# The values products moved up behind the scores in thirteen rows of a cross-attention and FFN kernel

## The chip, the cores and the metric

The kernel runs on one NeuronCore of a Trainium2 chip. The metric is the device time of one launch in microseconds (us), the median over the runs shown. TensorE (PE) multiplies, VectorE (DVE), ScalarE (ACT) and GpSimd (POOL) do the rest of the arithmetic, and transfers are issued from SyncE's queue (SP). Each engine works through its own list of instructions in order; semaphores tie the lists together.

## The reference

One decoder layer over 16 sequences of 64 tokens, 1024 tokens of width 512: cross-attention with 32 heads of 128, then a dense layer with a routed low-rank addition. Cut to what matters:

```python
q = (layernorm(x) @ Wq).reshape(b, 64, 32, 128)
k = (ctx @ Wk).reshape(b, 64, 32, 128)
v = (ctx @ Wv).reshape(b, 64, 32, 128)
score = einsum('bqhd,bkhd->bhqk', q, k) / sqrt(128) + position_bias
score = where(mask, score, -inf)
probs = where(mask, softmax(score), 0)
x = x + einsum('bhqk,bkhd->bqhd', probs, v).reshape(b, 64, 4096) @ Wo
h = layernorm(x)
x = x + h @ base_W.T + base_b + lora(h, top-k softmax of h @ router_W.T)
```

[...]

## The kernel before

**Precision and blocks.** A float32 operand is split into a high part (ACT casts it, L70) and a low part (DVE subtracts, L71), and each product is three matmuls: high by high, high by low, low by high. The three projections use Strassen-Winograd sums: seven products of halves in place of eight, in the order of `ORDER` = 1, 2, 6, 5, 7, 4, 3 (L37).

**Stages.** First the keys and values of all heads are computed and written to DRAM (up to about 320 us of the span). Then comes the attention loop over the 16 head pairs (`for p in range(NP)`, L607), here called rows: row p with p = 0 is the first. Last comes the dense layer (from L680).

**A row.** The program of a row is a string of letters, `steps` (L608), read from left to right:

- `S` (L617): the scores of the row's pair. For each of the two heads 16 matmuls of 128x64 tiles into a bank of their own pool (L470; the profile counts two records for each), then DVE adds the bias (L473) and takes the maxima (L475). In rows 1 to 14 that pair is p. The first head's exponentials, eight activations of 64 columns on ACT (L481), follow at once; the second head's are recorded at the fifth `Q`.
- `Q` (L625): one of the seven Winograd products of the next pair's queries, six matmuls of 512 columns (L259). Products 1, 6, 7 and 4 add up in one PSUM bank, called x; product 2 fills bank z, products 5 and 3 fill bank y. After products 1, 6 and 7 ACT copies bank x to SBUF (`u`, L554) before the next product is added onto it; after product 4 it copies the result out (L561). DVE forms the other three results (L565).
- `P` (L612): the values products of the pair before (`pv_mm`, L510): 64 matmuls of 64x64 tiles (128 records, L517) into four banks, from `pt`, the turned probabilities, and `v`. Each bank is split by ACT (cast to `oh`, L70) and DVE (`ol`, L71). The next four `v` tiles are loaded into the same buffers behind it.
- `O` (L671): one eighth of the output projection of that pair (`proj_o`, L527): six matmuls of 512 columns, then DVE adds the bank to `acc` (L534).
- `h` (L661): the second head's softmax is finished behind the last `O`: normed on DVE (L487 to L489), transposed on DVE (L498), copied by ACT to `pt` (L500), and four transfers put the off-diagonal quarters in place (L505). The first head's is finished at the fifth `Q`.

The fifth `Q` also loads the output weights for the next row (`load_o`, L448: `so` by DMA, split into `wh` on ACT and `wl` on DVE), and the seventh loads and splits the query weights for the pair after next (`gh`, `gl`).

**Order.** PE's list is the order of recording. The lists of ACT, DVE, POOL and SP are put together by a scheduler from the recording, its own estimates, `issue_after` (not ahead of a named instruction) and `high_priority(offset=SOON)`, which holds for the splits of the values banks, the copies of Winograd banks and the additions to `acc`. The general PSUM pool has six banks (L61), the pool of the scores two.

## Time and profile before

| | |
|---|---|
| median of 3 runs | 763.34 us (763.02 to 763.68) |
| profiled execution: span from the first to the last instruction | 761.7 us |
| between the span and the median | 1.6 us |
| PE, DVE, ACT, POOL busy | 752.5, 565.8, 412.0, 194.8 us |
| granted TensorE clock over the span | 0.999 |
| one row of the loop (537.93 to 562.83) | 24.90 us |

The profiled execution is known by its span alone; what lies around the span is taken as the 1.6 us by which the median exceeds it. A timeline line reads: start, duration, engine, source line, operation, output and inputs with their shapes, the count of merged instructions, and in brackets the idle time before it with what ended it. The duration of a matmul includes its way through the array, so that starts, not ends, show the rate: in a run of 512-column matmuls one starts every 0.227 us. The same holds on ACT and DVE, where the next instruction starts some 0.1 us before the former one's recorded end.

### The profile page before, as it was taken

The page shows a single profiled execution, that of the slowest core. Times are in us where ns is not written, and L with a number is a line of the kernel's source. Part 1 is how long each engine was busy: PE and PEld are TensorE (multiplying, and loading weights), DVE is VectorE, ACT ScalarE, POOL GpSimd, SP SyncE. Part 2 cuts the span into 40 slices and gives each one's busy share as a digit, 9 for nine tenths or more (in the row PEclk, how much of TensorE's full clock was granted, in tenths as well). Part 3 has the DMA queues.
Part 4 walks back from the last instruction along what each step waited for, and adds up shares of the span by engine and source line. Part 5 has one row for each costly group of instructions (what it writes and reads, how often), then busy time and mean ns, then how long its engine had stood idle before and what let it go on. Part 6 is the DMA issues. An engine that isn't in the chain of part 4 may idle for free.

```text
span 761.7 us, 16780 instructions
## 1 busy us (share of the span) xinstructions
PE 752.5 (99%) x6154; PEld 624.9 (82%) x6154; DVE 565.8 (74%) x1076; ACT 412.0 (54%) x1157; POOL 194.8 (26%) x271
## 2 busy tenths in 40 slices
PE   8999999999999999999999999999999999999998
PEld 6888888888788888877888888888888888888898
DVE  7986567666655776869778777787778777878975
ACT  5654444444444445667645565456645765474361
POOL 0000008108820693223220222022211232010330
PEclk9999999999999999999999999999999999999999
DMA  6685647465735446466554465436544564462011
GB/s 255 229 285 186 205 157 229 147 218 179 224 130 187 156 126 225 142 222 217 189 158 149 138 199 167 142 120 201 174 141 134 180 185 140 125 199 84 1 57 56
DMA packets 84946, 126.79 MB, mean 166 GB/s; under 512 B 11776, under 2 KB 35072, under 8 KB 84864
## 3 DMA queue, kind: packets, MB, share of 16 engines
q1 hardware_dynamic: 80624, 123.56, 49.9%
q0 software_dynamic: 4096, 2.11, 1.2%
q8 instruction: 48, 0.79, 0.5%
q14 instruction: 34, 0.28, 0.1%
q10 hardware_dynamic: 144, 0.06, 0.0%
HBM read 83.74 MB, written 35.65 MB: 157 GB/s over the span
## 4 chain that ended last, share of the span: by engine, by line
PE 91%; DVE 3%; POOL 2%; DMA 2%; issue 1%; ACT 0%; SPq 0%; DVEq 0%; ACTq 0%; POOLq 0%
PE ps L259 73%; PE yz L259 5%; PE ps L742 5%; PE ps L517 4%; PE pss L470 4%; POOL xT L333 1%; DMA cT<-in_ctxT 1%; DMA so<-in_wo 0%; DMA xT<-xb 0%; DVE bs L708 0%; DVE gl L71 0%; PE pt L104 0%; DVE s L161 0%; DVE ol L71 0%; POOL st L711 0%
## 5 line engine op out<-in xcount | busy, mean ns | idle before, releaser
L481 ACT ACTIVATE p<-p,nm 128x64 f32<-128x64 f32 x256 | 85.9, 339 | 33.3 <-DVE nm L475 31.0
L534 DVE TENSOR_TENSOR acc<-acc,ps 128x512 f32<-128x512 f32 x128 | 86.8, 681 | 21.2 <-PE ps L259 20.4
L259 PE MATMUL ps<-wh,ol 128*128 128x512 f32 x256 | 99.9, 390 | 0.8 <-DVE ol L71 0.8
L259 PE MATMUL ps<-wh,oh 128*128 128x512 f32 x256 | 100.1, 391 | 0.0
L259 PE MATMUL ps<-wl,oh 128*128 128x512 f32 x256 | 99.7, 389 | 0.0
L70 ACT CAST gh<-s 128x512 fp32r<-128x512 f32 (+1 forms) x128 | 64.4, 514 | 56.0 <-PE ps L259 45.7
L333 POOL DMA_DIRECT2D xT<-xb x128 | 69.7, 552 | 84.9 <-DVE xb L330 80.7
L71 DVE TENSOR_TENSOR gl<-s,gh 128x512 fp32r<-128x512 f32 (+1 forms) x128 | 72.0, 566 | 23.2 <-ACT gh L70 23.1
L161 POOL TENSOR_TENSOR s<-rq 128x256 f32<-128x256 f32 x32 | 25.3, 790 | 238.9 <-DMA rq<-in_wq 190.1
L71 DVE TENSOR_TENSOR ol<-ps,oh 128x512 fp32r<-128x512 f32 x64 | 39.9, 683 | 31.5 <-ACT oh L70 31.3
L70 ACT CAST gh<-raw 128x512 fp32r<-128x512 f32 x48 | 29.8, 623 | 52.8 <-PE yz L259 36.1
L259 PEld LDWEIGHTS ps<-wh,ol 128*128 128x128 f32 x256 | 48.1, 188 | 11.4 <-DVE ol L71 1.6
L259 PEld LDWEIGHTS ps<-wl,oh 128*128 128x128 f32 x256 | 48.1, 188 | 10.0
L259 PEld LDWEIGHTS ps<-wh,oh 128*128 128x128 f32 x256 | 48.0, 188 | 10.0
L71 DVE TENSOR_TENSOR gl<-raw,gh 128x512 fp32r<-128x512 f32 x48 | 35.1, 731 | 27.9 <-ACT gh L70 20.7
L461 POOL TENSOR_TENSOR bm<-bm,maskb 128x512 f32<-128x512 f32 x32 | 42.4, 1348 | 36.6 <-DMA bm<-in_fside 36.6
L481 ACT ACTIVATION_READ_ACCUMULATOR p<-p,nm 128x1 f32 x256 | 48.6, 190 | 0.0
L565 DVE TENSOR_TENSOR q<-u,ps 128x512 f32<-128x512 f32 x48 | 32.8, 683 | 20.4 <-PE ps L259 16.0
L70 ACT CAST oh<-ps 128x512 fp32r<-128x512 f32 x64 | 33.2, 590 | 11.0 <-PE ps L517 11.0
L70 ACT CAST gh<-rq 128x256 fp32r<-128x256 f32 x48 | 19.5, 406 | 36.0 <-PE ps L259 32.1
L517 PEld LDWEIGHTS ps<-pt,v 64*64 64x64 f32 x2048 | 31.9, 135 | 5.7 <-issue 5.6
L554 ACT COPY u<-ps 128x512 f32<-128x512 f32 x48 | 27.9, 581 | 15.9 <-PE ps L259 8.8
(258 smaller groups left out, 1986.2 us busy)
## 6 DMA issues: line engine op xcount, KB each, us to landing
kd<-c SPq DMA_DIRECT2D x64, 256.0 KB, 2.6
vd<-c SPq DMA_DIRECT2D x64, 256.0 KB, 2.8
kT<-kd SPq DMA_DIRECT2D x64, 256.0 KB, 3.9
v<-vd SPq DMA_DIRECT2D x64, 256.0 KB, 3.7
raw<-in_wk SPq DMA_DIRECT2D x32, 256.0 KB, 4.0
raw<-in_wv SPq DMA_DIRECT2D x32, 256.0 KB, 4.3
rq<-in_wq SPq DMA_DIRECT2D x32, 256.0 KB, 4.1
bm<-in_fside SPq DMA_DIRECT2D x32, 256.0 KB, 4.5
```

Of the source, the lines that this page charges most:

```text
L70: first = nc.scalar.copy(hi, src)
L71: return first, (lo_eng or nc.vector).tensor_tensor(lo, src, hi.bitcast(F32), ALU.subtract)
L259: nc.tensor.matmul(o, lhsT=a, rhs=b, start=first and n == 0, stop=last and n == 2, skip_group_check=True)
L333: nc.gpsimd.dma_start(out=dst[32 * j:32 * j + 32, :, 32 * i:32 * i + 32], in_=xb[32 * i:32 * i + 32, j])
L461: nc.gpsimd.tensor_tensor(bm, bm, maskb, ALU.add)
L470: nc.tensor.matmul(ps[a * S:(a + 1) * S, t, :], lhsT=qT[n // 8][:, cq], rhs=kT[m // 8][:, ck], start=True, stop=True)
L481: nc.scalar.activation(p[:, t, :], p[:, t, :], AF.Exp, bias=nm[:, t:t + 1], accum_out=sme[:, t:t + 1])
L517: nc.tensor.matmul(ps[a][d:d + S, t * S:(t + 1) * S], lhsT=v[t // 2][r, t % 2, c], rhs=pt[r, :, t, :], start=True, stop=True)
L534: return nc.vector.tensor_tensor(acc[:, t, :], acc[:, t, :], ps, ALU.add)
L554: copy = nc.scalar.copy(s[i], b["x"])
L565: add = nc.vector.tensor_tensor(self.blocks[key], s[u], b[bk], ALU.add)
L742: nc.tensor.matmul(o, lhsT=a, rhs=b, start=start, stop=stop, skip_group_check=True)
```

## The change

The strings of rows 2 to 14 (the third to the fifteenth) are new. Row 1 keeps the old string, rows 0 and 15 are not touched.

```diff
-                steps = ("QSQQQQQQt" if p == 0 else "SQQQPQQOOQOhOQOOOO" if p + 2 < NP else
-                         "SQQQPQQOQQfSeeOOOOOhh" if p + 1 < NP else "PooOOOOOOO")
+                steps = ("QSQQQQQQt" if p == 0 else "SQQQPQQOOQOhOQOOOO" if p == 1 else
+                         "SPQQQQOOQOhQOQOOOO" if p + 2 < NP else
+                         "SPQQQQQOQQfSeeOOOOOhh" if p + 1 < NP else "PooOOOOOOO")
```

`P` moves from behind the third `Q` to a place directly behind `S`. In rows 2 to 13 the fifth `Q` (product 7) moves behind two `O`, so that what hangs on it (the second head's exponentials, the first head's softmax, the output weights) is recorded later by two `O`. `h` still stands behind the third `O`, now with one `Q` fewer ahead of it, and the sixth and seventh `Q` stand behind it, each with an `O` after. In row 14 only `P` moves. The count of every letter in a row is unchanged.

On ACT the scheduler's order changes with it. Before, a row runs: four exponentials of the first head, the copy of product 1, four exponentials, the copy of product 6, four casts of the values banks, two of the output weights. After: six exponentials, a cast, an exponential, a cast, an exponential, two casts of the values banks, one cast of the output weights, and then the copy of product 1; the other cast of the output weights and the copy of product 6 follow. On SP the first transfer of output weights moves from ahead of the eight `pt` transfers to between the two groups of four.

## Prediction

> **What bounds the kernel now.** I read the page's busy shares first, then the chain of work that ended last in order of time, then the timelines of PE and ACT over one row, and last the one place where PE waited for a copy out of an accumulating bank.

> ```profile
> PE 752.5 (99%) x6154; PEld 624.9 (82%) x6154; DVE 565.8 (74%) x1076; ACT 412.0 (54%) x1157; POOL 194.8 (26%) x271
> ```
> ```profile
> 538.00 2.02 PE pss L470 x64
> 540.02 4.32 PE ps L259 x18
> 544.34 2.04 PE ps L517 x128
> 546.38 16.52 PE ps L259 x72
> ```

> PE is busy for 99% of the span, and the chain of a row holds PE work only: 24.90 us = 2.02 (`S`) + 4.32 (three `Q`) + 2.04 (`P`) + 16.52 (four `Q`, eight `O`). No other engine is on the path, so a row gets shorter only where PE itself loses time, and any PE wait lengthens it in full. Where PE loses time is seen in its timeline:

> ```profile
> 537.61 0.39 PE L259 MATMUL ps<-wl,oh 128*128 128x512 f32 x1
> 537.93 2.09 PE L470 MATMUL pss<-kT,q 128*64 128x64 f32 x64
> 539.95 0.50 PE L259 MATMUL ps<-t1h,gh 128*128 128x512 f32 x1
> 540.28 0.39 PE L259 MATMUL ps<-t1h,gl 128*128 128x512 f32 x1
> ...
> 543.95 0.39 PE L259 MATMUL ps<-t6l,gh 128*128 128x512 f32 x1
> 544.27 2.11 PE L517 MATMUL ps<-pt,v 64*64 64x64 f32 x128
> 546.31 0.50 PE L259 MATMUL ps<-t5h,gh 128*128 128x512 f32 x1
> 546.65 0.39 PE L259 MATMUL ps<-t5h,gl 128*128 128x512 f32 x1
> ```

> The usual step between starts is 0.227 us. Going into small tiles it is 0.32 (537.61 to 537.93, 543.95 to 544.27), so 0.09 is lost; coming out it is 0.33 or 0.34, so about 0.10 is lost. A row pays four such changes. Of ACT's list in the same row:

> ```profile
> 540.69 0.35 ACT L481 ACTIVATE p<-p,nm 128x64 f32<-128x64 f32 x1 [2.42 <-DVE nm L475]
> ...
> 542.04 0.56 ACT L554 COPY u<-ps 128x512 f32<-128x512 f32 x1
> ...
> 545.47 2.06 ACT L70 CAST oh<-ps 128x512 fp32r<-128x512 f32 x4 [0.45 <-PE ps L517]
> 547.41 1.15 ACT L70 CAST wh<-so 128x512 fp32r<-128x512 f32 x2
> ```

> The exponentials start 2.76 us after the row's first score (540.69 less 537.93) and wait only for the maxima. The copy of product 1 comes after four of them, at 542.04, and ends at 542.60, just ahead of product 6 at 542.80, which is added onto the same bank and may not start before. That edge of 0.20 us is the point of the whole change.

> ```profile
> 193.37 0.58 ACT L230 COPY u<-ps 128x512 f32<-128x512 f32 x1
> 193.99 0.50 PE L259 MATMUL ps<-t4h,gh 128*128 128x512 f32 x1 [1.34 <-ACT u L230]
> ```

> Here, in the keys' stage, PE did wait for such a copy. It started 0.04 us after the copy's end, and its second matmul came at 194.33, 0.34 later: a restart costs 0.11.

> **The change, part by part.** Times are from the row's first score.

> *`P` behind `S`, on PE.* One way out of small tiles (0.10) and one way in (0.09) go; the step from 128x64 to 64x64 tiles comes. The trace does not show that step. It lies between 0 (the steps inside each section lose nothing) and 0.20 (both edges); nearest is a way in, 0.09, which I take. `P` starts at 2.02 + 0.09 = 2.11, product 1 at 4.15 (2.04 later), and lasts 0.34 + 5 x 0.227 = 1.47; product 2 lasts 1.36. Product 6 is then due at 6.98.

> *The copy of product 1, on ACT.* Its bank is full at about 5.9, but in the new order six exponentials, four casts of values banks, two exponentials and one cast of output weights stand ahead of it. From the rows: exponentials 0.3375 each (four from 540.69 to 542.04), casts 0.485 each (four from 545.47 to 547.41), an output-weight cast 0.525 (two from 547.41 to the next ACT instruction at 548.46). Nothing in that list waits: the first bank of `P` is full at some 3.3 and its cast comes at 4.79; the third at 4.3 and 6.4; the output-weight cast needs product 1's weights free (5.5) and comes at 7.4. So 2.76 + 8 x 0.3375 + 4 x 0.485 + 0.525 = 7.93; the copy's 0.58 brings 8.51, PE starts at 8.55. Product 6 waits 8.55 - 6.98 = 1.57 us, and 0.11 for the restart. Behind that list wait DVE's result of product 2 (needs `u`), then the second low part of the output weights and the additions to `acc`; first use of any is after 11 us.

> *The rest of the row.* From product 6 on: 13 blocks (five `Q`, eight `O`) of 1.36 = 17.68, with 0.11 for the restart and 0.09 for the way into the next `S`: 8.55 + 17.88 = 26.43 us against 24.90, so +1.53. Where `P` starts does not enter this, as long as the copy comes late: what the merged tile sections save is eaten by the wait, which is why the unknown step has no weight in the sum. Lower end for the ACT part: `u` and exponential mixed take 0.46 (542.04 to 542.50) where I have 0.485 for a cast, and no restart loss: 4 x 0.025 + 0.11, +1.3. Upper end: casts at their whole recorded 0.59 (the last of the four): 4 x 0.105, +1.95.

> *The later copies.* Product 6 ends at 10.2, its copy follows an idle ACT; product 7 stands at 14.1 behind two `O`: no wait. Product 7's copy at 15.7, product 4 at 16.8: no wait.

> *The second head's turn.* Its exponentials now hang on product 7's copy and run from 16.2 to about 19.4 (eight, with the copy of product 4 between); norm on DVE at 20.5, transpose behind the last query result at 21.7, the copy to `pt` ends at 23.2. SP has by then issued the first head's four transfers (from 20.3) and one output-weight load. The second four go out at 0.59 each (four take 2.41 on SP's queue), the last at about 25.1; transfers of `pt` take 1.9 us at the median and 3.8 at most.

> ```profile
> DMA to landing us min/median/max: 1.7/1.9/3.8
> ```

> They land at 27.0 to 28.9; the next row's second half of `P` stands at 26.43 + 2.11 + 1.02 = 29.6. So 0.7 to 2.6 us are left, where the old order left over 5. `P` itself does not wait.

> *SP and POOL.* The `v` loads go out behind `P`, at 4.2 in place of 7.8, and land a row ahead of use. The key loads behind the output weights' low part go out a little sooner. The output-weight load now between the `pt` groups waits for a split at about 21 that is done before it is reached. POOL's list is unchanged; its sums wait for query weights that are issued at the same point of the row. All of this I cost at nothing; its cover is the row's remainder.

> *Sum.* Twelve rows and row 14, where the same ACT order stands, make 13 x 1.53 = 19.9. The profiled span is 761.7, so 781.6 plus 1.6 around it (the median's distance from the span) = 783.2 us.

> [...] Four tile changes a row at 0.09 to 0.10 are in the trace, and of the 128x64 to 64x64 step nothing is. [...]

> **The rivals.**

> *The merge pays, no wait comes (faster).* ACT would have to reach the copy by 6.98 - 0.62 = 6.36 instead of 7.93; from there on the wait is gone. The gain is then 0.10 a row by my step, 0 to 0.20 by its ends: 760.7 to 763.3, middle 762.0. For it: every piece of ACT work ahead is short, and ACT is busy 54% only. Against: between 540.69 and 548.46 its list is nearly without gaps, and it runs in order. 0.07.

> *The turn comes late as well (slower still).* If `pt` transfers take their longest 3.8 and SP is a further microsecond late, the second half of `P` waits some 0.3 us, up to 1 us with a cast or two in the way. `P` may wait 1.57 us before product 6 is held by it and not by the copy (8.55 - 6.98), and its third bank has 2 us to spare before its cast; up to there a late turn costs nothing, and beyond it up to 0.5 a row: 783 to 790. For it: the margin falls from over 5 us to about 1. 0.11.

> *The wait is made up elsewhere (no change).* The rest of each row has no PE wait to take it from. 0.02.

> **How the numbers follow.** The likeliest, 0.80, is 783.2, its own range 13 x 1.3 to 13 x 1.95 above 763.3, 780.2 to 788.7. Adding most of the late turn's cases gives 778 to 790. A measurement of this kernel tells about 0.2% (1.5 us) from no change. Faster 0.06, within 0.2% 0.03 (the merge may pay nothing, or the wait be made up), slower 0.91.

> **What the profile after would show.** A row of about 26.4 us. Product 6 (`t6h`, L259) with some 1.6 us idle before it, released by ACT's `u` L554, 13 times; no such line for product 7 or 4. ACT's copy starting some 5.2 us after the row's first exponential. The step from L470 to L517 against 0.09. No wait of L517 for `pt`. Wrong would be: rows of 24.7 (the copy in time), or PE held at L517 by a `pt` transfer, or by `v`.

## The result, and the profile after

The changed kernel takes 782.49 us (median of 4 runs, 782.2 to 783.69) against 763.34 (763.02 to 763.68): 1.0252 times, interval 1.0238 to 1.0267, so 19.15 us more. 783.2 had been forecast. The profiled execution has a span of 780.9 us at a granted clock of 0.998; the spans differ by 19.2.

The page's busy shares after:

```profile
PE 756.2 (97%) x6154; PEld 628.2 (80%) x6154; DVE 572.2 (73%) x1076; ACT 407.4 (52%) x1157; POOL 203.8 (26%) x271
```

PE has the same 6154 matmuls and is busy for 97% of a longer span, no longer 99%: PE itself has idle time now. Where that begins is in the chain of work that ended last, in order of time (start, duration, what), through one row:

```profile
442.27 1.11 PE pss L470 x32
...
443.47 0.70 DVE p L473
...
444.19 0.70 DVE nm L475
...
444.98 1.52 ACT p L481 x9
...
449.55 0.62 ACT wh L70
450.18 0.49 ACT u L554
450.67 0.04 issue
450.71 17.77 PE ps L259 x77
```

The chain of a row held only PE before. Now it leaves PE in the middle of the scores, goes over DVE's bias and maxima and through ACT's list (exponentials, casts, a weight cast) to the copy `u`, and comes back to PE at product 6. PE's timeline of the same row (start, duration, engine, line, operation, count, and in brackets the idle time and its releaser):

```profile
442.20 2.08 PE L470 MATMUL pss<-kT,q 128*64 128x64 f32 x64
444.22 2.22 PE L517 MATMUL ps<-pt,v 64*64 64x64 f32 x128
446.37 0.50 PE L259 MATMUL ps<-t1h,gh 128*128 128x512 f32 x1
...
448.97 0.39 PE L259 MATMUL ps<-t2l,gh 128*128 128x512 f32 x1
450.71 0.50 PE L259 MATMUL ps<-t6h,gh 128*128 128x512 f32 x1 [1.35 <-ACT u L554]
451.05 0.39 PE L259 MATMUL ps<-t6h,gl 128*128 128x512 f32 x1
```

From the last matmul of product 2 to the first of product 6 it is 450.71 - 448.97 = 1.74 us in place of 0.227. ACT's timeline says why:

```profile
444.98 0.35 ACT L481 ACTIVATE p<-p,nm 128x64 f32<-128x64 f32 x1 [2.44 <-DVE nm L475]
...
446.99 0.57 ACT L70 CAST oh<-ps 128x512 fp32r<-128x512 f32 x1
...
449.55 0.62 ACT L70 CAST wh<-so 128x512 fp32r<-128x512 f32 x1
450.07 0.58 ACT L554 COPY u<-ps 128x512 f32<-128x512 f32 x1
```

The copy starts 7.87 us after the row's first score (450.07 - 442.20). Its bank is full long before: product 1's last matmul starts at 447.61.

From the first score of row 2 to that of row 15 the trace of before takes 314.82 us and the trace after 334.50, so 19.68 more in the thirteen rows. What follows row 15's first score takes 83.7 in both, and row 2 starts 0.48 earlier after; that is the 19.2. Row lengths here and below are the distances between first scores in PE's timeline: rows 2 to 13 were 24.90 to 25.11, and are 26.41 to 26.43 in nine of the twelve (26.33, 26.79 and 26.69 in rows 2, 3 and 6). Row 14 went from 15.38 to 16.91.

The waits of PE between 362 and 690 us (waiting line, releaser, us in total, times, longest) hold one thing that I had not expected:

```profile
PE ps L259 <- ACT u L554: 11.3, 10, 1.5
PE ps L517 <- issue: 4.1, 4, 1.4
PE ps L259 <- issue: 1.2, 1, 1.2
```

Five times PE stood still in or just behind `P` with "issue" as the releaser: it waited for nothing that the profile shows. I call that a hold. In one such row, row 4:

```profile
417.80 1.65 PE L517 MATMUL ps<-pt,v 64*64 64x64 f32 x91
420.81 0.80 PE L517 MATMUL ps<-pt,v 64*64 64x64 f32 x37 [1.36 <-issue]
```

These holds cost nothing here, since PE would have waited for the copy a little later anyway, and the row stays at 26.41 (rows 3 and 6 are longer for another reason, given below). They matter as soon as the copy is in time.

### The profile page after: what moved, and what is told of

It reads as the page before. It is cut to its first block, busy times and chain, and to the rows that moved or that the text cites. A ratio compares the mean times of both kernels' runs of the same rounds, so it can differ in the third digit from the quotient of the medians.

```text
span 780.9 us, 16807 instructions
## 1 busy us (share of the span) xinstructions
PE 756.2 (97%) x6154; PEld 628.2 (80%) x6154; DVE 572.2 (73%) x1076; ACT 407.4 (52%) x1157; POOL 203.8 (26%) x271
## 3 DMA queue, kind: packets, MB, share of 16 engines
q0 software_dynamic: 4096, 2.11, 1.2%
## 4 chain that ended last, share of the span: by engine, by line
PE 83%; ACT 7%; DVE 4%; issue 2%; POOL 2%; DMA 1%; SPq 0%; DVEq 0%; ACTq 0%; POOLq 0%
PE ps L259 68%; PE yz L259 5%; PE ps L743 5%; ACT p L481 4%; PE pss L470 3%; PE ps L517 2%; ACT oh L70 2%; POOL xT L333 1%; DVE p L473 1%; DVE nm L475 1%; ACT wh L70 1%; DMA cT<-in_ctxT 1%; ACT u L554 1%; DMA xT<-xb 0%; DVE bs L709 0%
## 5 line engine op out<-in xcount | busy, mean ns | idle before, releaser
L481 ACT ACTIVATE p<-p,nm 128x64 f32<-128x64 f32 x256 | 86.3, 339 | 33.9 <-DVE nm L475 31.5
L259 PE MATMUL ps<-wh,oh 128*128 128x512 f32 x256 | 100.1, 391 | 0.0
L259 PE MATMUL ps<-wh,ol 128*128 128x512 f32 x256 | 99.8, 390 | 0.1
L259 PE MATMUL ps<-wl,oh 128*128 128x512 f32 x256 | 99.7, 389 | 0.0
L161 POOL TENSOR_TENSOR s<-rq 128x256 f32<-128x256 f32 x32 | 26.4, 825 | 243.5 <-DMA rq<-in_wq 177.5
L70 ACT CAST gh<-s 128x512 fp32r<-128x512 f32 (+1 forms) x128 | 64.2, 513 | 32.7 <-PE ps L259 22.8
L554 ACT COPY u<-ps 128x512 f32<-128x512 f32 x48 | 28.1, 585 | 63.4 <-PE ps L259 63.1
L71 DVE TENSOR_TENSOR ol<-ps,oh 128x512 fp32r<-128x512 f32 x64 | 42.4, 688 | 22.5 <-ACT oh L70 19.3
L461 POOL TENSOR_TENSOR bm<-bm,maskb 128x512 f32<-128x512 f32 x32 | 48.6, 1537 | 39.0 <-DMA bm<-in_fside 39.0
L70 ACT CAST gh<-raw 128x512 fp32r<-128x512 f32 x48 | 29.8, 622 | 53.1 <-PE yz L259 36.6
L259 PEld LDWEIGHTS ps<-wh,ol 128*128 128x128 f32 x256 | 48.1, 188 | 10.5 <-DVE ol L71 0.8
L259 PEld LDWEIGHTS ps<-wl,oh 128*128 128x128 f32 x256 | 48.1, 188 | 10.0
L259 PEld LDWEIGHTS ps<-wh,oh 128*128 128x128 f32 x256 | 48.0, 188 | 10.0
L481 ACT ACTIVATION_READ_ACCUMULATOR p<-p,nm 128x1 f32 x256 | 48.5, 189 | 0.0
L517 PE MATMUL ps<-pt,v 64*64 64x64 f32 x2048 | 36.8, 221 | 4.2 <-issue 4.1
L500 ACT COPY pt<-pb 128x512 f32<-128x512 f32 x32 | 19.9, 621 | 37.7 <-DVE pb L498 31.0
L517 PEld LDWEIGHTS ps<-pt,v 64*64 64x64 f32 x2048 | 34.0, 134 | 6.7 <-issue 5.4
```

Of the source, the lines that this page charges most:

```text
L70: first = nc.scalar.copy(hi, src)
L71: return first, (lo_eng or nc.vector).tensor_tensor(lo, src, hi.bitcast(F32), ALU.subtract)
L161: self.eng.tensor_tensor(r, a, b, op)
L259: nc.tensor.matmul(o, lhsT=a, rhs=b, start=first and n == 0, stop=last and n == 2, skip_group_check=True)
L461: nc.gpsimd.tensor_tensor(bm, bm, maskb, ALU.add)
L481: nc.scalar.activation(p[:, t, :], p[:, t, :], AF.Exp, bias=nm[:, t:t + 1], accum_out=sme[:, t:t + 1])
```

## The experiments

My theory: `P`'s new place puts ACT's copy of product 1 behind thirteen other pieces, and PE waits for it; the rest of the change costs nothing. Rivals: the moved fifth `Q` and the turn behind it cost something too; or the place of `P` costs by itself, whatever ACT does. The string letters are those of the section on the kernel before.

**Only `P` moved** (rows 2 to 13 keep the fifth `Q` in its old place; row 14 as changed):

```diff
-                         "SPQQQQOOQOhQOQOOOO" if p + 2 < NP else
+                         "SPQQQQQOOQOhOQOOOO" if p + 2 < NP else
```

> Rows 2 to 13 with the values products behind the scores, the rest of the row as in the kernel before (fifth query product ahead of two output blocks, turn of the second head at its old place); row 14 as in the changed kernel. Theory (the copy of product 1 stands behind exponentials and casts on ACT): that order on ACT is the same as in the changed kernel, so product 6 waits as long: 782.5 us, within 1.5. Rival (the later fifth product and the moved turn make the loss): 763, as those parts are undone.

Measured: 781.91 us, ratio 1.022 (1.019 to 1.0251); rows of 26.33 to 26.45 (row 3: 26.76), row 14 16.89, and PE waits for `u` ten times, 11.1 us. The whole loss is there without the moved turn.

**Only the rest** (`P` stays behind the third `Q`, the fifth `Q` moves behind two `O`):

```diff
-                         "SPQQQQOOQOhQOQOOOO" if p + 2 < NP else
-                         "SPQQQQQOQQfSeeOOOOOhh" if p + 1 < NP else "PooOOOOOOO")
+                         "SQQQPQOOQOhQOQOOOO" if p + 2 < NP else
+                         "SQQQPQQOQQfSeeOOOOOhh" if p + 1 < NP else "PooOOOOOOO")
```

> The other half alone: values products at their old place, fifth query product and turn as in the changed kernel in rows 2 to 13, row 14 as before. Theory: ACT reaches the copy of product 1 after four exponentials as in the kernel before, no wait: 763.3 us, within 1.5. Rival (the later turn and the later product 7 cost time): 770 to 782.

Measured: 763.71 us, ratio 0.9993 (0.9977 to 1.0009). Rows of 24.90 to 24.98, but for row 2, which is 25.39 long and has one hold of 0.59; PE waits for no `pt` transfer. The later turn costs nothing that this run can tell.

**A cast less ahead of the copy** (the changed kernel; the output weights' casts may not go ahead of product 1's copy):

```diff
-                            with tc.issue_after(evicted[0].ins), tc.issue_after(evicted[1].ins):
+                            with (tc.issue_after(evicted[0].ins), tc.issue_after(evicted[1].ins),
+                                  tc.issue_after(nxt.first)):
```

> The changed kernel with one thing moved: the cast of output weights that stands ahead of the copy of product 1 on ACT comes behind it. Theory: ACT reaches the copy 0.53 us sooner, each row is 0.53 shorter where the copy sets it; in about four rows PE is also held in the values products for 1.2 to 1.4 us without a waited-for engine, and these gain at most 0.3: 782.5 - (9 x 0.53 + 4 x 0.3) = 776.5 us. Rival (the late copy is only a sign of something else, for instance the transfers of the turned probabilities): no change, 782.5.

Measured: 777.39 us, ratio 1.0174 (1.0133 to 1.0214). Rows that nothing else disturbs are 25.90 long, 0.52 less than 26.42: one weight cast of 0.525 in the sum is worth just that. Row 3 of the profiled execution, however, is 29.53 long, with a hold of 3.08 us in `P`, and that execution took 781.69 us where the other three took 776.88 to 777.8; so this run says less in its total than in its rows.

**The copy in time** (the changed kernel; the first head's exponentials are recorded behind product 1's copy, not behind `S`; the edit covers rows 2 to 14, one more than its expectation says):

```diff
-                        if p == ns - 1:
+                        if p == ns - 1 and not 1 < p < NP - 1:
                             exps_of(1)
...
+                        if n == 1 and 1 < p < NP - 1:
+                            with tc.issue_after(nxt.first):
+                                exps_of(1)
```

> The changed kernel with the first head's exponentials behind the copy of product 1 on ACT in rows 2 to 13. Theory: no wait of product 6 in these rows, one of 1.5 left in row 14. If nothing else holds PE, rows of about 24.8: 763.3 + 1.5 - 12 x 0.1 = 763.6 us. If the unexplained holds of 1.2 to 1.4 us in the values products stay, they are no longer covered by the wait: four or five of them add 5 to 6.5, 769 us, and PE shows them with 'issue' as what ended them, near a transfer of the instruction queue. Rival (the wait for the copy was not the cause): 780 or more.

Measured: 767.94 us, ratio 1.004 (1.0022 to 1.0059). PE's waits between 362 and 690 us:

```profile
PE ps L517 <- issue: 3.7, 5, 1.8
PE ps L259 <- issue: 0.9, 1, 0.9
PE pss L470 <- DVE q L565: 0.2, 1, 0.2
```

No wait for `u` is left, and 14.6 of the 19.15 us are gone (782.49 - 767.94). So the copy was the cause. But it isn't 762: six rows are 24.76 or 24.77 long, 0.17 below the 24.94 of before, and the six others 25.23 to 28.47. Those are the rows with holds, which the wait had covered in the changed kernel. In the worst, row 3, PE's timeline is:

```profile
388.36 2.15 PE L517 MATMUL ps<-pt,v 64*64 64x64 f32 x120
392.27 0.35 PE L517 MATMUL ps<-pt,v 64*64 64x64 f32 x8 [1.76 <-issue]
392.55 0.50 PE L259 MATMUL ps<-t1h,gh 128*128 128x512 f32 x1
...
394.24 0.63 PE L259 MATMUL ps<-t2h,gh 128*128 128x512 f32 x1
394.67 0.63 PE L259 MATMUL ps<-t2h,gl 128*128 128x512 f32 x1
```

PE stops eight records ahead of `P`'s end, and from 393.83 to 397.23 its steps are 0.41 to 0.43 in place of 0.227.

**What the holds are.** New theory: PE's own instructions run out. The page of the changed kernel shows instructions that come by DMA, in a queue of their own (packets, MB, share of 16 engines):

```profile
q8 instruction: 48, 0.79, 0.4%
```

That is 48 transfers of 16 KB each. PE has 12,308 recorded instructions, as many weight loads as matmuls (6154 each), so 12,308 / 48 = 256.4 to a transfer, if all of these are PE's. Scores and values in a row are 64 + 128 matmul records with as many weight loads, 384 instructions in 4.17 us (442.20 to 446.37), 92 per us; in the 512-column stretches it is two per 0.227 us, 8.8 per us. Every hold comes behind such a transfer: the one of row 4 above, at 420.81, behind a transfer that starts at 418.49 and lasts 0.96 (418.4 to 419.5 us, DMA of that window):

```profile
q8 instruction: 1, 0.02, 5.5%
```

Rivals: the early `P` itself, its data or a load of that row stops PE; or the moved exponentials do.

**The exponentials behind the copy, in the old strings** (control; the same edit, but with the strings of before):

```diff
                steps = ("QSQQQQQQt" if p == 0 else "SQQQPQQOOQOhOQOOOO" if p + 2 < NP else
                         "SQQQPQQOQQfSeeOOOOOhh" if p + 1 < NP else "PooOOOOOOO")
...
+                        if n == 1 and 1 < p < NP - 1:
+                            with tc.issue_after(nxt.first):
+                                exps_of(1)
```

> The old strings, with the first head's exponentials put behind the copy of product 1 in rows 2 to 14, as in the run before, but P behind the third Q. It is the control for that move on ACT. My theory: the copy was in time anyway and the exponentials' results are needed late, so 763.3 us (762 to 765), rows of 24.9 and no PE wait. If the move of the exponentials itself costs or brings something, the rows differ from 24.9 and the held rows of the run before (28.5, 25.9) turn up here too, 766 or more.

Measured: 764.3 us, ratio 0.9999 (0.9982 to 1.0015). Rows are 24.88 to 24.95, but for 26.40 (row 2) and 26.95 (row 7) in the profiled execution, each with one hold behind or in `P` (1.57 and 2.03). So the moved exponentials cost nothing in the mean, and the rival with them falls; but the expected absence of holds did not come out: the old form is held now and then too. In the trace of before it isn't.

**The transfers shifted by two rows** (the run with the copy in time, and 52 unused matmuls of 64 columns before the first stage):

```diff
+            for _ in range(52):
+                nc.tensor.matmul(warm[:, 0:64], lhsT=zero[:, 0:P], rhs=zero[:, 0:64], start=True, stop=True)
```

> The run with the exponentials behind the copy, and 52 further matmuls of 64 columns before the first stage, whose result nothing uses: with their weight loads 104 more instructions of PE. A row has 564 of PE's instructions, two 16 KB transfers' worth (256 each, if one takes 64 bytes) and 52 more, so 104 move the transfers by two rows. If those transfers of PE's instructions set the holds, rows 3, 4, 7, 8, 12 and 13 are no longer the held ones, but rows 2, 5, 6, 10 and 11 (and 1, which has the old string). If the holds come from the data, the loads or the row's own work, rows 3, 4, 7, 8, 12 and 13 stay the held ones. The total says little.

Measured: 768.04 us in one run. The rows of this and of the runs that follow, in us (bold: over 25.2 in rows 2 to 13; row 3 of the seven-row version has the old form and no hold, it loses 0.22 ahead of product 6):

| row | 2 | 3 | 4 | 5 | 6 | 7 | 8 | 9 | 10 | 11 | 12 | 13 | 14 |
|---|---|---|---|---|---|---|---|---|---|---|---|---|---|
| copy in time | 24.77 | **28.47** | **25.23** | 24.77 | 24.77 | **25.92** | **25.86** | 24.76 | 24.77 | 24.77 | **25.48** | **25.40** | 15.25 |
| shifted | **25.53** | 24.83 | 24.77 | 24.83 | **26.19** | 24.77 | 24.83 | 24.83 | **26.57** | **26.39** | 24.83 | 24.77 | 16.03 |
| seven rows | 24.83 | **25.27** | 24.90 | 24.83 | 24.77 | 24.88 | 24.93 | 24.77 | 24.81 | 24.77 | 24.97 | 24.90 | 15.31 |
| the other six | **25.79** | **27.54** | **26.25** | 24.93 | 24.90 | **25.57** | **25.85** | 25.01 | 24.96 | 24.90 | **26.93** | **25.99** | 15.44 |
| seven, shifted | **25.40** | 25.03 | 24.94 | 24.77 | **26.29** | 25.14 | 24.90 | 24.83 | **29.05** | **26.20** | 24.97 | 24.90 | 15.29 |

The six held rows are free and rows 2, 6, 10 and 11 are held: four of the five that had been named, row 5 not. Row 14, which had not been named, is held as well, by 0.82 between products 1 and 2. Data and loads of a row are the same as before, so they aren't the cause.

The count of PE's instructions says it more sharply. I counted the records from the start of the trace to the end of each hold: matmuls, weight loads, and the semaphore instructions on PE's list, some four to six a row. With the copy in time the holds end at 4545, 5057, 6849, 7361, 9665 and 10177; the distances are 512, 1792, 512, 2304 and 512, which is 2, 7, 2, 9 and 2 times 256, without a remainder. In the shifted run rows 2, 6, 10, 11 and 14 are held at 4033, 6337, 8641, 9153 and 10945: 9, 9, 2 and 7 times 256. All 40 stops of 0.4 us or more with "issue" as the releaser in the loops of the twelve traces, old strings or new, end at 193 more than a multiple of 256. So do two that the profile puts down to DVE, the one of row 14 here and one below. So PE stops at fixed places of its list, one transfer's worth apart.

Where such a place lies in a row decides: with the copy in time the held rows have it 306 to 398 records behind the first score (row 3: 374, being 64 + 120 matmuls, twice, and 6 semaphore instructions); a free row has its places at 282 or below and at 422 or above. So the merged rows of these traces were held where somewhat more than 256 small instructions, and hardly any of the long ones, stood ahead of the place; in the control run, where `P` stands alone, its 245 to 258 records ahead of the place were enough twice, and in the trace of before they were not. In the shifted run row 5 has the place at 411 (its scores start at 5414, the place is at 4033 + 7 x 256), and it was free. A row has 570 records with the semaphore instructions, 2 x 256 + 58, so that two rows make 116, and my 104 did not quite make them up.

The timing fits. In the run of the other six rows, below, the transfer for row 13 starts when 125 records are still ahead of the hold, lands 0.92 us later, and PE goes on 1.3 us after that. In the 512-column stretch 125 instructions last some 14 us, in small tiles 1.4. In all these 42 holds PE goes on 1.2 to 1.6 us after such a transfer has landed. That it is the transfer which PE waits for is inferred from these times and from the places; no record of the profile names it.

**One product between** (the copy in time, but one `Q` stands between `S` and `P`):

```diff
-                         "SPQQQQOOQOhQOQOOOO" if p + 2 < NP else
-                         "SPQQQQQOQQfSeeOOOOOhh" if p + 1 < NP else "PooOOOOOOO")
+                         "SQPQQQOOQOhQOQOOOO" if p + 2 < NP else
+                         "SQPQQQQOQQfSeeOOOOOhh" if p + 1 < NP else "PooOOOOOOO")
```

> The run with the exponentials behind the copy, but P stands behind the first Q in rows 2 to 14, so that six matmuls of 512 columns lie between S and P. If PE is held because 384 instructions of small tiles follow each other in 4.1 us and use up what is fetched of its list, the 1.4 us between give time to fetch: no holds or much shorter ones, rows of 24.9 and 763.3 us (762.5 to 765). If the holds come from somewhere else, such as the early P itself, they remain, and it takes 767 or so.

Measured: 765.39 us, ratio 1.0015 (1.0 to 1.003), 0.4 above the end of what was expected, though well below 767.94. One hold is left, 0.87 in row 7, and ten of the twelve rows are 25.02 to 25.07: 0.1 above before. That 0.1 is in `P`:

```profile
440.48 2.27 PE L517 MATMUL ps<-pt,v 64*64 64x64 f32 x128
442.68 0.50 PE L259 MATMUL ps<-t2h,gh 128*128 128x512 f32 x1
```

`P` takes 2.20 here and 2.15 in most other rows, where it took 2.04 before. Row 14 has a short wait for a copy as well (0.4) and is 16.16 long.

**Seven rows** (`P` directly behind `S` and the exponentials behind the copy only in rows 2, 5, 6, 9, 10, 11 and 14, which were not held; the other rows as before):

```diff
+            OLD = (1, 3, 4, 7, 8, 12, 13)
...
-                steps = ("QSQQQQQQt" if p == 0 else "SQQQPQQOOQOhOQOOOO" if p == 1 else
-                         "SPQQQQOOQOhQOQOOOO" if p + 2 < NP else
+                steps = ("QSQQQQQQt" if p == 0 else "SQQQPQQOOQOhOQOOOO" if p in OLD else
+                         "SPQQQQQOOQOhOQOOOO" if p + 2 < NP else
...
-                        if p == ns - 1:
+                        if p == ns - 1 and (p in OLD or p + 1 == NP or p == 0):
...
+                        if n == 1 and p not in OLD and 0 < p < NP - 1:
+                            with tc.issue_after(nxt.first):
+                                exps_of(1)
```

> P directly behind S and the first head's exponentials behind the copy, but only in the seven rows 2, 5, 6, 9, 10, 11 and 14, the rows that were not held in the full version; rows 3, 4, 7, 8, 12 and 13 are as in the kernel before, and the fifth Q stays in its old place. If the holds hang on where the transfers of PE's instructions fall, which the order of the rows does not move, the seven rows have none and each is 0.17 us shorter: 763.3 - 7 x 0.17 = 762.1 us. If a held row were only a matter of how many merged rows stand one behind the other, or of time, some of the seven are held and it takes 764 us or more.

Measured: 761.48 us (760.92 to 762.75, 12 runs), ratio 0.997 (0.9958 to 0.9982) to the kernel before, whose 29 runs beside it have a median of 763.75. It beats both kernels. The waits of PE between 362 and 690 us are down to one line, as in the trace of before:

```profile
PE pss L470 <- DVE q L565: 0.2, 1, 0.2
```

The seven rows hold the 1.2 us that I expected, to within what a row can tell (24.77 to 24.83 against 24.94, 15.31 against 15.38: 0.9 in sum). That the medians are 2.3 apart is more than that. In the profiled executions the spans differ by 2.2 (759.5 and 761.7): 0.9 of it lies in rows 2 to 14, and 1.06 in row 1 (26.87 against 27.93), whose string is the old one in both. Over the twelve traces row 1 takes 26.27 to 28.19, so less than half of this gain is shown to come from the merged rows. The kernel before also spreads further in these runs (762.1 to 767.72), perhaps from holds of its own as in the control run; that is not shown.

**The other six rows** (the seven-row version, but with the merged form only in rows 3, 4, 7, 8, 12 and 13, row 14 as before):

```diff
-            OLD = (1, 3, 4, 7, 8, 12, 13)
+            OLD = (1, 2, 5, 6, 9, 10, 11, 14)
...
-                steps = ("QSQQQQQQt" if p == 0 else "SQQQPQQOOQOhOQOOOO" if p in OLD else
+                steps = ("QSQQQQQQt" if p == 0 else "SQQQPQQOOQOhOQOOOO" if p in OLD and p + 2 < NP else
...
-                         "SPQQQQQOQQfSeeOOOOOhh" if p + 1 < NP else "PooOOOOOOO")
+                         "SQQQPQQOQQfSeeOOOOOhh" if p + 1 < NP else "PooOOOOOOO")
```

> The counterpart of the seven rows: P directly behind S and the exponentials behind the copy only in rows 3, 4, 7, 8, 12 and 13, the old form in all others. If the holds belong to these rows because PE's instructions are transferred there, they are all back: the full version stood at 767.9, which is 763.3 less 7 x 0.17 for the free rows plus 5.8 for these, so here it takes 763.3 + 5.8 = 769 us (766.5 to 770). If any merged row is as good as any other and the seven rows were only fewer, six make 762.3 us.

Measured: 771.34 us, ratio 1.0088 (1.006 to 1.0115). All six are held, and one row of the old form, row 2. One merged row fewer than in the seven-row version, and 1.0088 in place of 0.997, some 9 us: which rows are merged decides. The size was 1.3 above the range: the holds end at the very places of the list where they ended with the copy in time (4545 to 10177), but they are longer, up to 2.72 us. Their length goes with how late the transfer of instructions starts: with 0, 33, 117, 125 and 187 records still ahead of the place (rows 3, 12, 4, 13 and 8) the hold in `P` is 2.72, 2.12, 1.45, 1.19 and 1.02 us, and in the run with the copy in time 64 and 231 records ahead (rows 3 and 4) go with 1.98 and 0.42. What makes a transfer start early or late stays open.

**Seven rows, shifted** (the seven-row version with the 52 unused matmuls at the start):

```diff
+            for _ in range(52):
+                nc.tensor.matmul(warm[:, 0:64], lhsT=zero[:, 0:P], rhs=zero[:, 0:64], start=True, stop=True)
```

> The seven-row version (2, 5, 6, 9, 10, 11, 14) with the 52 unused matmuls at the start, which move the transfers of PE's instructions by two rows and change nothing else in the loop. If the transfers decide, rows 2, 6, 10 and 11 of the seven are held now, by 0.7 to 1.8 us each as in the shifted run of the full version, so 761.5 + 4 x 1.2 = 766 us (764 to 768). If it doesn't matter where the transfers fall, the gain stays: 761.5 us, with the 52 small matmuls ahead of all work at some 0.5 us at most.

Measured: 768.63 us, ratio 1.0045 (1.0022 to 1.0068): 52 small matmuls ahead of everything turn 0.997 into 1.0045, some 6 us. Rows 2, 6, 10 and 11 are held, as named, and no other of the seven. It is 0.6 more than the range. In the profiled execution (769.79) row 10 alone loses more than that:

```profile
565.90 2.22 PE L519 MATMUL ps<-pt,v 64*64 64x64 f32 x128
570.79 0.79 PE L259 MATMUL ps<-t1h,gh 128*128 128x512 f32 x1 [2.66 <-DVE ol L71]
571.38 0.63 PE L259 MATMUL ps<-t1h,gl 128*128 128x512 f32 x1
```

The profile puts this one down to DVE, whose last split ended 0.5 us before; but it ends at record 8641, on the same grid as the others of its run (4033, 6337, 8641, 9153: 9, 9 and 2 times 256), and 1.5 us after a transfer of instructions has landed. I take it for a hold of the same kind.

## Why the prediction was right

- *The copy of product 1, on ACT.* The decisive step. The list came out in the order and at the pace that were summed: the exponentials start 2.78 us after the first score (2.76 forecast), the copy at 7.87 (7.93), product 6 at 8.51 (8.55). Product 6 was due at 448.97 + 0.227, 7.00 into the row (6.98), so it is 1.51 late (1.57), and the restart of 0.34 costs 0.11 as said. Shown by the two runs that take pieces out of that list: one weight cast less, 0.52 less; the exponentials out of the way, no wait.
- *The rest of the row.* 26.43 forecast, 26.41 to 26.43 in nine rows. Rows 3 and 6 are 0.3 to 0.4 longer because the exponentials start late, 3.13 and 3.06 after the first score; in row 6 DVE has an addition to `acc` and a low part of the query weights ahead of the bias. 13 x 1.53 = 19.9 against 19.68 in the trace.
- *`P` behind `S`, on PE.* The step from 128x64 to 64x64 tiles was taken as 0.09, between 0 and 0.20. `P` starts 2.02 after the first score (444.22 - 442.20), not 2.11: `S` takes as long up to `P` as it took up to a query product (539.95 - 537.93). That is not a free step, though. The last score record to the next section takes 0.15 in both traces, where one pair of score records follows another by 0.058; the 2.02 contain that. And `P` lasts 2.15 in place of 2.04. The same 2.15 stands where a query product lies between, so these 0.11 are not the price of that step; what they are stays open. Of the two changes that go (0.10 and 0.09) some 0.08 is left, and rows without wait or hold are 0.11 shorter than the control's (24.77 against 24.88): about one change of the four, not two. It had no weight in the sum, as said.
- *The later copies, SP and POOL, the second head's turn.* No wait at product 7 or 4, none for `pt` or `v`, and 763.71 us with the turn moved alone. The last `pt` transfer goes out 25.2 us into the row (25.1 forecast), and the slowest in that row takes 2.5 to land, within the time that was left. The rival of a late turn did not come about.
- *Thirteen waits at product 6* were named; the trace books ten to `u`, since in rows 4, 7 and 8 a hold had made PE late already. Chain and row length are the same.

One step failed, in the rival that the merge pays: "from there on the wait is gone. The gain is then 0.10 a row by my step", 760.7 to 763.3. With the copy in time it is 767.94. The gain per row was right, but the working took PE for busy or waiting on an engine, and had no term for PE's own instructions: 384 small ones in a row. It was also not among the signs that would show the prediction wrong. The forecast was saved from it by the wait, which came behind the holds and was longer; that was luck, since no term of the sum stood for them. Where the copy is in time, that working is 5 to 7 us too low and has the wrong sign.

## What to carry to other kernels

When a stretch of work is moved up on the bounding engine, list what that puts ahead of each in-order copy which feeds the engine back, and add up that list: 13 pieces of 0.3 to 0.5 us were the whole answer here. Behind a wait there may be a second, shorter one that it covers, so a fix should be priced by running it. And count TensorE's instructions per us: here 384 small ones ran at 92 per us, a 16 KB transfer brought some 256, and in some rows PE stood still. What helped here was to spread them (one product between: 765.39 us in place of 767.94) or to merge only the rows that were not held (761.48).

## What the runs showed of the hardware

```profile
385.00:389.50 4.50, 4.50 (x143) 3.92 (x141) 3.64 (x7) 0.81 (x2) 0.00 (x0) 1.00 0.46 156
394.00:397.20 3.20, 3.20 (x9) 2.46 (x8) 1.45 (x4) 3.10 (x14) 3.20 (x4) 0.50 0.87 294
397.50:400.50 3.00, 3.00 (x15) 2.47 (x14) 0.40 (x2) 1.90 (x7) 1.02 (x1) 1.00 0.21 80
```

  Half speed for 3.4 us adds some 1.7 us to a hold of 1.98. The hold of 2.88 in row 10 of the shifted seven-row version has the same behind it (0.50 from 571.4 to 573.9), and so has the one of 3.08 in row 3 of the run with a cast less ahead (0.50 from 397.68 to 401.09), but the one of 2.72 in row 3 of the other six rows does not (1.00 from 394.0 to 397.4). So the length of the pause alone does not decide. The traces speak for where it falls: within a trace the granted clock changes only at times that lie a whole number of 3.413 us apart (with the copy in time at 4.72, 393.84, 397.25 and 765.89). On that grid PE is idle for 1.76, 2.52 and 2.73 us of the stretch just ahead of the three halvings, and the pause of 2.72 lies across a border, 1.44 us ahead of it and 1.06 behind. The most idle time of a stretch in any of the loops that no halving follows is 1.69. By these figures I estimate that the halving comes with somewhere between 1.69 and 1.76 us of idle time in one such stretch; three halvings are few to rest that on.
